# A static planner's engine costs: occupancy apart from latency, with new stage times and a blocked key layout

## The chip, the core and the metric

The kernel runs on one core of a Trainium2 chip. The metric is the device time of one execution in microseconds; before the change it is 1197.02 us, the median of three runs (1195.31 to 1197.02).

## What is computed

The input `x` has 4 sequences of 512 tokens with 128 channels, float32 throughout. Six residual blocks follow each other:

```python
x = x + 0.5 * rwkv_mix(layernorm(x))            # three 128x128 matmuls, token shift, sigmoid, relu^2
x = x + attention(layernorm(x))                 # 16 heads of 64, 512x512 scores, relative bias, softmax
x = x + 0.5 * rwkv_mix(layernorm(x))
x = x + 0.5 * local_transformer(layernorm(x))   # 2 layers
x = x + gated_recurrence(layernorm(x))          # a scan along the tokens, layer norm inside
x = x + 0.5 * local_transformer(layernorm(x))
```

A layer of `local_transformer` is an attention in windows of 64 tokens (8 heads of 64; each query block of 64 sees its own and the previous block: 128 keys), with l2-normalised and rotated q and k, then a feed-forward of 128 to 2 x 341 to 128 with a gelu gate.

## The kernel before

**Work.** Everything is tiled to 128 partitions. The global attention is cut into 32 units, a pair of heads times a sequence (`unit`, L559): q, k and v projections, 4 query tiles of scores, softmax, transposes of the probabilities (one head by TensorE and a ScalarE copy, the other by VectorE, a DRAM buffer and DMAs), the weighted values, and the output projection. A `local_stage` (L877) is one local transformer on one sequence; each of its two layers has 4 token tiles that pass through `rotate`, `values`, `turn`, `soften`, `turn_back`, `weigh`, `turn_outputs` and `project` (L683 to L834), and then `feed_forward`. Each of the 4 sequences has two local stages with a `recurrence` between them and ends in `leave` (transpose, copy, store).

**The key tile.** `turn` (L727) transposes q and k of a token tile with TensorE and copies them out of PSUM with ScalarE. The keys lie in `kT`, [channel, head pair, 64 + 128 tokens]: the first 64 are the previous tile's last 64, brought by one DMA from SBUF to SBUF per tile (48 in all), 4 runs of 64 floats on each partition. `soften` (L746) multiplies each query block of 64 with a run of 128 keys, 16 small matmuls (64x64 weights, 128 columns) to a tile. It then adds the mask (VectorE), takes the maximum (VectorE), subtracts it (GpSimd) and takes the exponential (ScalarE).

**What sets the order.** No instruction is issued as the program is written down. Each is recorded (`Recorder`, L294) as an `Op` with a cost and a due time `vt`; `Plan.plan` (L175) then lays all 5791 ops out, engine by engine, in a greedy list schedule, and `emit` writes them in that order, pinned. The schedule takes the engine that can start first; among the ops that can start on it then, it takes the one with the smallest due time. Ops due later than HORIZON after the oldest unplanned one are passed over. A change of TensorE's tile mode (full array; "row" pairs for the scores; "col" pairs for the weighted values) adds MODE_BIAS to the due time, a change of ScalarE's function table TABLE_BIAS. Buffers (8 PSUM banks, 33 SBUF pairs) are given out in the same walk. So costs and due times decide nothing but the order: the hardware waits on semaphores, whatever the plan thought.

The due times come from a few stage constants on L53 and L54. ATTN is where the units begin; a unit follows the last by 4 STEPs, its later parts are LATER steps behind. LATE is where the local stages begin; TURN is the stride from one turn of a sequence to its next, and the sequences follow each other by LAG turns. The costs come from `Recorder.cost` (L331). In the planner before, an op's cost does two things at once:

```python
free[op.engine] = op.done = at + cost
```

The engine is free, and the result is there, at the same moment.

Of the kernel before, what the change touches and what calls it, by code (L numbers as in the profile page):

```python
# [8 lines left out]
AF = mybir.ActivationFunctionType  # L9
ALU = mybir.AluOpType  # L10
# [4 lines left out]
P = 128  # L15
# [34 lines left out]


PAIRS = 33
STEP, TURN = 3.6, 11.7  # L53
ATTN, LATE, LAG, LATER = 20.5, 400.0, 4.5, 7.7  # L54

class Tile:

# [53 lines left out]
class Op:  # L111
    def __init__(self, engine, vt):
        self.engine, self.vt = engine, vt
        self.calls, self.tiles, self.preds, self.succs = [], [], set(), []
        self.cost, self.mode, self.table, self.bytes = 0.0, None, None, 0
        self.start = self.done = None


class Plan:
# [1 line left out]

    LATENCY, HORIZON, SWITCH, TABLE = 0.07, 31.7, 0.1, 1.28
    IDLE, COLD, FIRST = 2.5, 8.0, 6
    MODE_BIAS, TABLE_BIAS = 10.5, 10.3

    def __init__(self, tc, memory):
        self.tc, self.nc, self.memory = tc, tc.nc, memory
# [45 lines left out]
    def plan(self):  # L175
        for op in self.ops:
            for t in op.tiles:
                t.left += 1
            for p in op.preds:
                p.succs.append(op)  # L180
        for op in reversed(self.ops):
            for s in op.succs:
                op.vt = min(op.vt, s.vt - s.cost)
        waiting = {op: len(op.preds) for op in self.ops}
        ready = {}
        for op in self.ops:
            if not op.preds:
                ready.setdefault(op.engine, []).append((0.0, op))
        free, mode, order, wire, cold = {}, "full", [], 0.0, 0.0
        unplanned = sorted(self.ops, key=lambda o: -o.vt)  # L190
        table = self.FIRST
        while unplanned:
            while unplanned and unplanned[-1].start is not None:
                unplanned.pop()
            if not unplanned:
                break
            horizon = unplanned[-1].vt + self.HORIZON
            best = None
            for engine, ops in ready.items():
                now, able = free.get(engine, 0.0), []  # L200
                for at, op in ops:
                    if op.vt > horizon:
                        continue
                    at = max(at, now)
                    new = [t.kind for t in op.tiles if t.kind != "fixed" and t.slot is None]
                    for kind in set(new):
                        at = max(at, self.memory.when(kind, new.count(kind)))
                    able.append((at, op))
                if not able:
                    continue  # L210
                first = min(a for a, _ in able)
                if best is not None and first >= best[0]:
                    continue
                if first == float("inf"):
                    continue

                def key(x):
                    k = x[1].vt
                    if engine == "tensor" and x[1].mode != mode:
                        k += self.MODE_BIAS  # L220
                    if x[1].table and x[1].table != table:
                        k += self.TABLE_BIAS
                    return k

                at, op = min((x for x in able if x[0] <= first + 0.05), key=key)
                best = (first, at, op)
            if best is None:
                raise RuntimeError("the plan finds no place for anything that is left")
            _, at, op = best
            self.memory.now = at  # L230
            for t in op.tiles:
                if t.kind != "fixed" and t.slot is None:
                    self.memory.take(t)
            op.start, cost = at, op.cost
            if op.engine == "tensor":
                if op.mode != mode:
                    cost, mode = cost + self.SWITCH, op.mode

                if at - free.get("tensor", -self.IDLE) >= self.IDLE:
                    cold = at + self.COLD  # L240
                cost += min(cost, max(0.0, cold - at) / 2)
            if op.table and op.table != table:
                cost, table = cost + self.TABLE, op.table
            free[op.engine] = op.done = at + cost
            if op.bytes:
                wire = max(wire, op.done) + op.bytes / 250e3
                op.done = wire + 2.0
            ready[op.engine] = [x for x in ready[op.engine] if x[1] is not op]
            order.append(op)
            for t in op.tiles:  # L250
                t.left -= 1
                t.end = max(t.end, op.done)
                if not t.left and t.kind != "fixed":
                    self.memory.give(t)
            for s in op.succs:
                waiting[s] -= 1
                if not waiting[s]:
                    at = max(p.done + (self.LATENCY if p.engine != s.engine or p.bytes else 0.0) for p in s.preds)
                    ready.setdefault(s.engine, []).append((at, s))
        return order  # L260
# [33 lines left out]
class Recorder:  # L294
# [36 lines left out]
    def cost(self, name, outs, ins, kw, n):  # L331
# [8 lines left out]
            n = max(v.size() for v in (ins if name == "tensor_reduce" else outs) or outs)  # L340
        if self.engine == "vector":
            if name == "tensor_tensor_scan":
                return 1.22
            if name == "tensor_scalar":
                return 0.15 + 0.0006 * n
            inside = n > 256 and all(v.tile.kind != "S" for v in ins)
            return 0.15 + 0.00105 * n + (0.08 if "accum_out" in kw else 0.0) + 0.3 * inside
        if self.engine == "scalar":
            return 0.12 + 0.0009 * n + (0.32 if "accum_out" in kw else 0.0 if name == "copy" else 0.07)
        if name == "memset":  # L350
            return 0.1 + 0.0008 * n
        return 0.12 + 0.0022 * n + 0.12 * (n == T)


class Memory:
# [63 lines left out]
def tile_macaron(ctx: ExitStack, tc: tile.TileContext, i: dict, out: bass.AP):  # L419
# [47 lines left out]
    def vec(col, n=P):  # L467
        return vecs[:n, col : col + 1]
# [52 lines left out]
    def attention(wo, tdram):  # L521
# [37 lines left out]
        def unit(n, at):  # L559
# [26 lines left out]
            for q in range(NT):  # L586
# [14 lines left out]
                for j in range(2):  # L601
# [7 lines left out]
                    )  # L609
                dve.reciprocal(sm, sm)  # L610
                pool_.tensor_tensor(
                    e, e, sm.unsqueeze(2).to_broadcast([P, 2, T]), ALU.mult, cost=1.92
                )


# [61 lines left out]
    def local_attention(l, h):  # L677
# [5 lines left out]
        def rotate(t):  # L683
# [18 lines left out]

            s3 = sq.rearrange("p (h d) -> p h d", d=DH)
            sh = plan.tile("half", [P, 2 * H1, half])
            pool_.tensor_tensor(sh, s3[:, :, :half], s3[:, :, half:], ALU.add, cost=1.25)
            dve.tensor_reduce(rn, sh, AX.X, ALU.add)

            act.activation(rn, rn, AF.Relu, bias=tiny[:, 0:1])
# [2 lines left out]
            for lo, hi in ((slice(0, half), slice(half, DH)), (slice(half, DH), slice(0, half))):  # L711
                pool_.tensor_tensor(u4[..., lo], u4[..., lo], w4[..., hi], ALU.add, n=INNER)
            u3 = u.rearrange("p (h d) -> p h d", d=DH)
            pool_.tensor_tensor(
                u3, u3, rn.unsqueeze(2).to_broadcast([P, 2 * H1, DH]), ALU.mult, cost=1.94
            )
            us[t] = u

# [8 lines left out]
        def turn(t):  # L727

            u = us.pop(t)
            qTs[t] = plan.tile("half", [P, H1 // 2, P])  # L730

            if t == 0:
                kTs[t] = plan.tile("pair", [P, H1 // 2, WIN + P])
                pool_.memset(kTs[t][:, :, :WIN], 0.0)
            for g, dst in enumerate((qTs[t], kTs[t][:, :, WIN:])):
                ptp = plan.tile("S", [P, H1 // 2, P])
                with plan.bundle(0.44):
                    for pr in range(H1 // 2):
                        c = g * INNER + pr * P
                        pe.transpose(ptp[:, pr, :], u[:, c : c + P], ident)  # L740
                act.copy(dst, ptp, n=T)
            if t + 1 < NT:
                kTs[t + 1] = plan.tile("pair", [P, H1 // 2, WIN + P])
                dma.dma_start(out=kTs[t + 1][:, :, :WIN], in_=kTs[t][:, :, P:])

        def soften(t):  # L746

# [3 lines left out]
            with plan.bundle(0.9, "row"):  # L751
                for pr in range(H1 // 2):
                    for j in range(2):
                        hp = slice(j * DH, (j + 1) * DH)
                        for blk in range(2):
                            c = slice(blk * WIN, (blk + 1) * WIN)
                            pe.matmul(
                                sc[j][c, pr, :], lhsT=qT[hp, pr, c],
                                rhs=kT[hp, pr, blk * WIN : blk * WIN + KEYS], start=True, stop=True,
                            )  # L760
            e = plan.tile("pair", [P, H1, KEYS])
            mask = mask_sb[:, 0 if t == 0 else 1, :].unsqueeze(1).to_broadcast([P, H1 // 2, KEYS])
            for j in range(2):
                dve.tensor_tensor(
                    e[:, j * (H1 // 2) : (j + 1) * (H1 // 2), :], sc[j], mask, ALU.add
                )
            mx = plan.tile("small", [P, H1])
            dve.tensor_reduce(mx, e, AX.X, ALU.max)
            pool_.tensor_tensor(
                e, e, mx.unsqueeze(2).to_broadcast([P, H1, KEYS]), ALU.subtract, cost=1.92  # L770
            )
            act.activation(e, e, AF.Exp)
            es[t] = e

        def turn_back(t):
# [138 lines left out]
    def recurrence(b):  # L914
# [10 lines left out]
        sg = plan.tile("half", [P, T])  # L925
        act.activation(sg, pzh[1], AF.Sigmoid, bias=vec(V_BH))
        ra = plan.tile("half", [P, T])
        dve.tensor_scalar(ra, pzh[1], vec(V_BH), 0.0, ALU.add, ALU.max, cost=0.69)
        dve.scalar_tensor_tensor(ra, sg, 0.5, ra, ALU.min, ALU.add)
        pool_.tensor_tensor(z, z, ra, ALU.mult)  # L930
        plan.step()
# [211 lines left out]
```

## Time and profile before

| | us |
|---|---|
| median of three runs | 1197.02 |
| the profiled execution | 1196.85 |
| its span, first to last instruction | 1195.0 |
| PE busy | 1166.0 |
| VectorE (DVE) busy | 931.7 |
| ScalarE (ACT) busy | 868.1 |
| GpSimd (POOL) busy | 834.6 |

Almost every instruction has the line L313, the recorder's `issue`, so groups have to be told apart by their tiles and shapes. `psS` is a PSUM bank, `pair` any half or whole SBUF work buffer, `small` a small column buffer, `va` and `via` the values and the DRAM buffers. `PEld` is the weight load of a matmul. A float32 matmul stands in the trace as two records, a transpose as one. A matmul's end is modelled, so that PE reads as busy while it may be waiting: times of matmuls are best read from start to start. On the other engines a record runs from the start of an instruction to its last write, and the next one can start before that end.

TensorE's first matmul of an attention unit is at 32.5 us and its last at 498.2; the local stages begin at 406.5, with recurrences between them, and the last sequence's feed-forward and `leave` end the program.

### The profile page before, as it was taken

How to read it: one execution, taken by the hardware profiler on the slowest of the kernel's cores; microseconds unless marked ns; L12 is line 12 of the kernel's file. 1: busy time of each engine (PE TensorE's matmuls, PEld its weight loads, DVE VectorE, ACT ScalarE, POOL GpSimd, SP SyncE). 2: the span in 40 equal slices, each digit the busy share in tenths (PEclk: the TensorE clock that was granted, in tenths of full speed). 3: DMA queues.
4: the chain of work that ended last, by engine and by line, in shares of the span. 5: the costliest groups of instructions: out<-in, count | busy, mean ns of one | idle time of the engine just before them, and what ended most of it. 6: DMA issues, size and time to landing. Idle time of an engine off the chain costs nothing.

```text
span 1195.0 us, 25706 instructions
## 1 busy us (share of the span) xinstructions
PE 1166.0 (98%) x9356; PEld 721.2 (60%) x9356; DVE 931.7 (78%) x1995; ACT 868.1 (73%) x1745; POOL 834.6 (70%) x591
## 2 busy tenths in 40 slices
PE   8999999999999999999999999999999999999996
PEld 3455556565555555567577766664576676776763
DVE  5778778778788787888888787877888888787853
ACT  5887667667676777777777687777877777677772
POOL 4756646656556787999898685726989998786720
PEclk9999999999999999999999999999999999999998
DMA  5276876686885742322021111100121112011100
GB/s 138 92 204 201 247 216 197 199 231 210 227 244 179 227 120 85 89 47 55 14 56 24 45 24 24 45 2 9 28 47 23 42 33 51 15 41 37 41 24 18
DMA packets 98194, 114.97 MB, mean 96 GB/s; under 512 B 33850, under 2 KB 77540, under 8 KB 98068
## 3 DMA queue, kind: packets, MB, share of 16 engines
q1 hardware_dynamic: 97780, 113.24, 33.8%
q8 instruction: 75, 1.23, 0.4%
q14 instruction: 51, 0.42, 0.1%
q10 hardware_dynamic: 288, 0.08, 0.0%
HBM read 57.41 MB, written 43.05 MB: 84 GB/s over the span
## 4 chain that ended last, share of the span: by engine, by line
PE 85%; DVE 7%; POOL 3%; issue 2%; ACT 2%; DMA 1%; SPq 0%; POOLq 0%; DVEq 0%; ACTq 0%
PE psS L313 85%; DVE pair L313 5%; POOL pair L313 3%; ACT pair L313 2%; DVE xT L313 1%; DVE small L313 1%; ACT L283 0%; DMA pair<-in_x_dram 0%; DMA pair<-via 0%; DVE w L313 0%; SPq L313 0%; POOLq L1139 0%; ACT small L313 0%; POOLq L313 0%; DVEq L313 0%
## 5 line engine op out<-in xcount | busy, mean ns | idle before, releaser
L313 POOL TENSOR_TENSOR pair<-pair,small 128x1024 f32<-128x1024 f32 x256 | 484.4, 1907 | 208.3 <-DVE small L313 168.2
L313 ACT COPY pair<-psS 128x512 f32<-128x512 f32 (+1 forms) x518 | 284.0, 590 | 136.5 <-PE psS L313 122.6
L313 PE MATMUL psS<-pair,pair 64*64 64x128 f32 (+4 forms) x4508 | 370.5, 300 | 2.3 <-ACT pair L313 1.0
L313 PEld LDWEIGHTS psS<-pair,pair 128*64 128x64 f32 (+2 forms) x4508 | 246.9, 140 | 116.6 <-issue 33.7
L313 PEld LDWEIGHTS psS<-ident,pair 128*128 128x128 f32 x1808 | 210.4, 142 | 117.5 <-issue 87.8
L313 POOL TENSOR_TENSOR pair<-pair,pair 128x512 f32<-128x512 f32 (+1 forms) x177 | 226.3, 1294 | 73.7 <-ACT pair L313 62.1
L313 PE MATMUL psS<-ident,pair 128*128 128x128 f32 x1808 | 248.4, 276 | 8.3 <-DMA pair<-in_x_dram 4.8
L313 ACT ACTIVATE pair<-pair,small 128x512 f32<-128x512 f32 x256 | 181.9, 712 | 43.7 <-DVE small L313 39.7
L313 DVE CUSTOM_DVE_ANT_0 pair<-psS,pair 128x512 f32<-128x512 f32 x256 | 164.7, 684 | 40.5 <-PE psS L313 40.1
L313 PE MATMUL psS<-wqkv,pair 128*128 128x512 f32 x384 | 185.6, 600 | 0.3 <-DVE pair L313 0.2
L313 POOL TENSOR_TENSOR pair<-pair 128x512 f32<-128x512 f32 x87 | 109.5, 1261 | 58.7 <-ACT pair L313 50.1
L313 ACT ACTIVATE pair<-pair 128x512 f32<-128x512 f32 (+1 forms) x152 | 122.3, 812 | 33.6 <-DVE pair L313 16.8
L313 PE MATMUL psS<-pair,w 128*128 128x512 f32 (+2 forms) x288 | 132.0, 604 | 3.8 <-POOL pair L313 3.5
L313 PE MATMUL psS<-pair 64*128 64x512 f32 (+2 forms) x548 | 128.0, 589 | 0.0
L313 DVE TENSOR_REDUCE small<-pair 128x16 f32<-128x512 f32 (+1 forms) x128 | 120.2, 948 | 6.2 <-POOL pair L313 4.0
L313 DVE TENSOR_TENSOR pair<-psS,cos 128x512 f32<-128x512 f32 x128 | 87.5, 684 | 37.0 <-PE psS L313 22.8
L313 ACT ACTIVATE pair<-psS 128x512 f32<-128x512 f32 x144 | 81.8, 596 | 45.5 <-PE psS L313 20.4
L313 PEld LDWEIGHTS psS<-wqkv,pair 128*128 128x128 f32 x384 | 65.4, 190 | 52.0 <-issue 42.9
L313 DVE TENSOR_TENSOR pair<-psS,sin 128x512 f32<-128x512 f32 x128 | 87.1, 681 | 11.4 <-ACT pair L313 11.3
L313 PEld LDWEIGHTS psS<-pair,w 128*128 128x128 f32 (+2 forms) x288 | 51.4, 185 | 67.2 <-issue 53.9
L313 DVE TENSOR_TENSOR pair<-psS,mask 128x512 f32<-128x512 f32 x128 | 82.6, 684 | 12.0 <-PE psS L313 8.0
L313 DVE STREAM_TRANSPOSE pair<-pair 128x512 f32<-128x512 f32 x128 | 87.5, 697 | 4.5 <-POOL pair L313 2.6
(71 smaller groups left out, 1183.6 us busy)
## 6 DMA issues: line engine op xcount, KB each, us to landing
via<-pair SPq DMA_DIRECT2D x64, 512.0 KB, 3.0
pair<-via SPq DMA_DIRECT2D x256, 128.0 KB, 3.5
pair<-va SPq DMA_DIRECT2D x112, 130.0 KB, 2.4
table<-tdram SPq DMA_DIRECT2D x16, 511.5 KB, 6.9
pair<-table SPq DMA_DIRECT2D x16, 448.0 KB, 5.2
pair<-pair SPq DMA_DIRECT2D x48, 128.0 KB, 2.3
wqkv<-in_L_ffn_wqkv_dram SPq DMA_DIRECT2D x2, 768.0 KB, 6.5
pair<-in_x_dram SPq DMA_DIRECT2D x4, 256.0 KB, 3.6
```

The source lines that it names most:

```text
L313: real(*[a.resolve() if isinstance(a, View) else a for a in args], **{k: a.resolve() if isinstance(a, View) else a for k, a in kw.items()},)
```

## The change

The planner now has two numbers for an op of VectorE, ScalarE and GpSimd: `cost`, for which the engine is held, and a TAIL after it, until which the result isn't there. The cost formulas of these engines are new, the explicit costs too, and so are eight stage constants (STEP, TURN, ATTN, LATE, LAG, LATER, HORIZON, TABLE_BIAS). Apart from the order, one thing that is executed changes: the key tile is kept in blocks of 32 tokens, [channel, block, head pair, 32], so that the previous tile's last 64 keys are one run of 256 floats on each partition. The key copy writes, and the score matmul reads, 4 runs of 32 floats where it was one of 128. `mx` is named earlier in the program and `scale=1.0` is written out at an exponential. The number of instructions of each engine stays what it was, but for ScalarE's table loads, which the order decides.

```diff
-STEP, TURN = 3.6, 11.7
-ATTN, LATE, LAG, LATER = 20.5, 400.0, 4.5, 7.7
+STEP, TURN = 3.5, 9.982
+ATTN, LATE, LAG, LATER = 14.455, 401.778, 3.886, 9.94
...
-    LATENCY, HORIZON, SWITCH, TABLE = 0.07, 31.7, 0.1, 1.28
+    LATENCY, HORIZON, SWITCH, TABLE = 0.07, 33.081, 0.1, 1.28
...
+    TAIL = {"vector": 0.085, "scalar": 0.115, "gpsimd": 0.05}
-    MODE_BIAS, TABLE_BIAS = 10.5, 10.3
+    MODE_BIAS, TABLE_BIAS = 10.5, 10.538
...
-            free[op.engine] = op.done = at + cost
+            free[op.engine] = at + cost
+            op.done = at + cost + self.TAIL.get(op.engine, 0.0)
...
             if name == "tensor_tensor_scan":
-                return 1.22
-            if name == "tensor_scalar":
-                return 0.15 + 0.0006 * n
-            inside = n > 256 and all(v.tile.kind != "S" for v in ins)
-            return 0.15 + 0.00105 * n + (0.08 if "accum_out" in kw else 0.0) + 0.3 * inside
+                return 1.2
+            psum = any(v.tile.kind == "S" for v in ins)
+            lo, hi = (outs + ins)[0].region()[0]
+            if name == "tensor_tensor_reduce":
+                return 0.078 + 0.00104 * n
+            inside = len(ins) > 1 and n > 256 and not psum
+            return 0.064 + 0.00104 * n + 0.09 * (hi - lo <= 64) + 0.06 * (len(ins) > 2) + 0.3 * inside
         if self.engine == "scalar":
-            return 0.12 + 0.0009 * n + (0.32 if "accum_out" in kw else 0.0 if name == "copy" else 0.07)
+            if name == "copy":
+                return 0.04 + 0.00083 * n
+            wide = len(ins) > 1 or any(v.tile.kind != "S" for v in ins)
+            return 0.05 + 0.00083 * n + 0.09 * wide + 0.06 * ("accum_out" in kw)
...
-        return 0.12 + 0.0022 * n + 0.12 * (n == T)
+        return 0.1 + 0.0022 * n
...
-                    e, e, sm.unsqueeze(2).to_broadcast([P, 2, T]), ALU.mult, cost=1.92
+                    e, e, sm.unsqueeze(2).to_broadcast([P, 2, T]), ALU.mult, cost=1.86
...
+            def keys():
+                return plan.tile("pair", [P, 2 + NQ, H1 // 2, QU])
             if t == 0:
-                kTs[t] = plan.tile("pair", [P, H1 // 2, WIN + P])
-                pool_.memset(kTs[t][:, :, :WIN], 0.0)
+                kTs[t] = keys()
+                pool_.memset(kTs[t][:, :2], 0.0)
...
+            act.copy(
+                kTs[t][:, 2:].rearrange("p a h u -> p h a u"),
+                ptp.rearrange("p h (a u) -> p h a u", u=QU), n=T,
+            )
             if t + 1 < NT:
-                kTs[t + 1] = plan.tile("pair", [P, H1 // 2, WIN + P])
-                dma.dma_start(out=kTs[t + 1][:, :, :WIN], in_=kTs[t][:, :, P:])
+                kTs[t + 1] = keys()
+                dma.dma_start(
+                    out=kTs[t + 1][:, :2].rearrange("p a h u -> p (a h u)"),
+                    in_=kTs[t][:, NQ:].rearrange("p a h u -> p (a h u)"),
+                )
...
-                                rhs=kT[hp, pr, blk * WIN : blk * WIN + KEYS], start=True, stop=True,
+                                rhs=kT[hp, blk * 2 : blk * 2 + 4, pr, :], start=True, stop=True,
```

The other explicit costs of GpSimd go from 1.92 to 1.86, 1.94 to 1.86 and 1.25 to 1.12, and an explicit 0.69 of a VectorE op gives way to the formula.

More of the change, by code (lines that the diff above doesn't have):

```diff
@@ L114, in __init__ @@
         self.calls, self.tiles, self.preds, self.succs = [], [], set(), []
-        self.cost, self.mode, self.table, self.bytes = 0.0, None, None, 0
+        self.cost, self.mode, self.table, self.bytes, self.tail = 0.0, None, None, 0, 0.0
         self.start = self.done = None
 class Plan:
-    LATENCY, HORIZON, SWITCH, TABLE = 0.07, 31.7, 0.1, 1.28
+    LATENCY, HORIZON, SWITCH, TABLE = 0.07, 33.081, 0.1, 1.28
     IDLE, COLD, FIRST = 2.5, 8.0, 6
-    MODE_BIAS, TABLE_BIAS = 10.5, 10.3
+    TAIL = {"vector": 0.085, "scalar": 0.115, "gpsimd": 0.05}
+    MODE_BIAS, TABLE_BIAS = 10.5, 10.538
     def __init__(self, tc, memory):
@@ L704, in rotate @@
             sh = plan.tile("half", [P, 2 * H1, half])
-            pool_.tensor_tensor(sh, s3[:, :, :half], s3[:, :, half:], ALU.add, cost=1.25)
+            pool_.tensor_tensor(sh, s3[:, :, :half], s3[:, :, half:], ALU.add, cost=1.12)
             dve.tensor_reduce(rn, sh, AX.X, ALU.add)
@@ L714, in rotate @@
             pool_.tensor_tensor(
-                u3, u3, rn.unsqueeze(2).to_broadcast([P, 2 * H1, DH]), ALU.mult, cost=1.94
+                u3, u3, rn.unsqueeze(2).to_broadcast([P, 2 * H1, DH]), ALU.mult, cost=1.86
             )
@@ L730, in turn @@
             qTs[t] = plan.tile("half", [P, H1 // 2, P])
+            def keys():
+                return plan.tile("pair", [P, 2 + NQ, H1 // 2, QU])
             if t == 0:
-                kTs[t] = plan.tile("pair", [P, H1 // 2, WIN + P])
-                pool_.memset(kTs[t][:, :, :WIN], 0.0)
[L735 to L741, printed above, removed]
-            if t + 1 < NT:
-                kTs[t + 1] = plan.tile("pair", [P, H1 // 2, WIN + P])
-                dma.dma_start(out=kTs[t + 1][:, :, :WIN], in_=kTs[t][:, :, P:])
+                kTs[t] = keys()
+                pool_.memset(kTs[t][:, :2], 0.0)
+            ptp = plan.tile("S", [P, H1 // 2, P])
+            with plan.bundle(0.44):
+                for pr in range(H1 // 2):
+                    pe.transpose(ptp[:, pr, :], u[:, pr * P : (pr + 1) * P], ident)
+            act.copy(qTs[t], ptp)
+            ptp = plan.tile("S", [P, H1 // 2, P])
+            with plan.bundle(0.44):
+                for pr in range(H1 // 2):
+                    c = INNER + pr * P
+                    pe.transpose(ptp[:, pr, :], u[:, c : c + P], ident)
+            act.copy(
+                kTs[t][:, 2:].rearrange("p a h u -> p h a u"),
+                ptp.rearrange("p h (a u) -> p h a u", u=QU), n=T,
+            )
+            if t + 1 < NT:
+                kTs[t + 1] = keys()
[3 more added lines that the diff above has]
+                )
         def soften(t):
@@ L758, in soften @@
                                 sc[j][c, pr, :], lhsT=qT[hp, pr, c],
-                                rhs=kT[hp, pr, blk * WIN : blk * WIN + KEYS], start=True, stop=True,
+                                rhs=kT[hp, blk * 2 : blk * 2 + 4, pr, :], start=True, stop=True,
                             )
             e = plan.tile("pair", [P, H1, KEYS])
-            mask = mask_sb[:, 0 if t == 0 else 1, :].unsqueeze(1).to_broadcast([P, H1 // 2, KEYS])
+            mask = mask_sb[:, 0 if t == 0 else 1, :]
+            mx = plan.tile("small", [P, H1])
+            mask = mask.unsqueeze(1).to_broadcast([P, H1 // 2, KEYS])
             for j in range(2):
@@ L766, in soften @@
                 )
-            mx = plan.tile("small", [P, H1])
             dve.tensor_reduce(mx, e, AX.X, ALU.max)
             pool_.tensor_tensor(
-                e, e, mx.unsqueeze(2).to_broadcast([P, H1, KEYS]), ALU.subtract, cost=1.92
+                e, e, mx.unsqueeze(2).to_broadcast([P, H1, KEYS]), ALU.subtract, cost=1.86
             )
-            act.activation(e, e, AF.Exp)
+            act.activation(e, e, AF.Exp, scale=1.0)
             es[t] = e
@@ L927, in recurrence @@
         ra = plan.tile("half", [P, T])
-        dve.tensor_scalar(ra, pzh[1], vec(V_BH), 0.0, ALU.add, ALU.max, cost=0.69)
+        dve.tensor_scalar(ra, pzh[1], vec(V_BH), 0.0, ALU.add, ALU.max)
         dve.scalar_tensor_tensor(ra, sg, 0.5, ra, ALU.min, ALU.add)
```

## The prediction

> **What bounds the kernel.** I read the page first.
>
> ```profile
> span 1195.0 us, 25706 instructions
> ...
> PE 1166.0 (98%) x9356; PEld 721.2 (60%) x9356; DVE 931.7 (78%) x1995; ACT 868.1 (73%) x1745; POOL 834.6 (70%) x591
> ...
> PE   8999999999999999999999999999999999999996
> ...
> POOL 4756646656556787999898685726989998786720
> PEclk9999999999999999999999999999999999999998
> ...
> PE 85%; DVE 7%; POOL 3%; issue 2%; ACT 2%; DMA 1%; SPq 0%; POOLq 0%; DVEq 0%; ACTq 0%
> ```
>
> TensorE carries the chain, but its 98% is not 98% of its peak, since a matmul's end is modelled. So I took the trace's starts. Undisturbed, a 128x512 record starts 0.429 us after the last (1108 of them, 475.3 us), a transpose 0.110 (1824, 199.7), a 128x128 record 0.111 (768, 85.2); of the tiled bundles a score pair takes 0.858 (128, 109.8), the local scores of a tile 0.874 (64, 55.9), eight weighted-value matmuls 1.727 (64, 110.5), eight local ones 0.466 (128, 59.6); the bias matmuls 2.6. Sum 1098.9 us. Each unbroken run of tiled bundles costs 0.15 to 0.20 more (a single score pair takes 1.059 to the next start, four take 3.634, so 0.20 is fixed): 35 score runs, 39 weighted, 41 local-score (0.16) and 39 local-weighted runs (0.15), 25.3 us. With 4.2 us to the first matmul and 4.1 after the last, 1132.5. The other 62.5 us are waits of TensorE: up to 75 us 10.4; between 375 and 525, where units give way to local stages, 10.5; between 750 and 925, where recurrences give way to the second local stages, 14.8; from 1100 on 12.8; elsewhere small ones, 14.0 in all.
>
> The end, in order of time (start, us, engine, operation, tiles, idle time before):
>
> ```profile
> 1170.63 1.05 PE L313 MATMUL psS<-pair,wo 128*128 128x128 f32 x8
> ...
> 1172.38 1.13 PE L313 MATMUL psS<-pair,ones 128*128 128x512 f32 x2
> ...
> 1175.02 1.12 PE L313 MATMUL psS<-pair,ones 128*128 128x512 f32 x2 [1.51 <-ACT pair L313]
> ...
> 1177.70 1.26 POOL L313 TENSOR_TENSOR pair<-pair,pair 128x512 f32<-128x512 f32 x1 [16.71 <-ACT pair L313]
> ...
> 1179.02 10.58 PE L313 MATMUL psS<-pair,w 128*128 128x512 f32 x18 [2.88 <-POOL pair L313]
> ...
> 1190.44 0.66 PE L313 MATMUL psS<-ident,xT 128*128 128x128 f32 x4 [0.85 <-DVE xT L313]
> ```
>
> One sequence is alone: after its last projection (1170.63) the two layer-norm matmuls, GpSimd's multiply and the feed-forward wait for one another. The clock falls as well, as the view by stretches shows (PE, PEld, DVE, ACT, POOL busy, granted clock):
>
> ```profile
> 1178.00:1185.00 7.00, 5.98 (x8) 2.43 (x9) 0.00 (x0) 2.81 (x4) 0.96 (x1) 0.55 0.00 0
> ```
>
> At 0.55 six records stand 0.857 apart, not 0.429: 2.6 us.
>
> **The premise.** Is an engine free before its result is there? First the group of ScalarE's copies (count, busy, mean ns), then two of them in order of time:
>
> ```profile
> L313 ACT COPY pair<-psS 128x512 f32<-128x512 f32 x516 | 282.9, 590 | 136.4 <-PE psS L313 122.6 <-DVE pair L313 6.1 <-DVE small L313 5.1
> ```
>
> ```profile
> 212.97 1.07 ACT L313 COPY pair<-psS 128x512 f32<-128x512 f32 x2 [2.72 <-PE psS L313]
> ```
>
> One copy takes 590 ns, two in a row 1.07 us: the second starts 0.48 after the first. The old formula holds ScalarE for 0.58 us, the new one for 0.465 with a result at 0.58. By starts likewise, VectorE's 128x512 from PSUM lasts 0.684 and is followed after 0.598 (old 0.688, new 0.596 + 0.085); GpSimd's 128x512 after 1.23 (old 1.37, new 1.23 + 0.05), its 128x1024 after 1.85 (old 1.92, new 1.86). The new costs are what this trace shows. They save no engine time; they decide which op the planner believes it can place next, and the gain can only come out of the 62.5 us of waits and 25.3 us of mode runs.
>
> **Part by part**, from the order of the changed program; a position is TensorE's work so far at the rates above, and another engine's work is counted between the TensorE steps that the plan puts it among. The counts of PE, DVE, POOL and SP instructions are equal (5592, 1997, 596, 571); so the 1098.9 us stay.
>
> *Mode runs.* 35, 39, 41, 39 become 33 score, 33 weighted, 38 local-score and 35 local-weighted runs: 2 x 0.20 + 6 x 0.15 + 3 x 0.16 + 4 x 0.15 = 2.4 us less on TensorE. It is the bound, so nothing covers that.
>
> *The end.* Before, the order behind the last projection is the other sequence's leave, layer norm, layer norm, six feed-forward matmuls, w2, leave: 10.3 us of TensorE work, all but 0.44 of it one chain. Now the last projection stands 7.7 us of work earlier (position 1080.1 of 1099, not 1087.8), and between the layer norm's two matmuls lie six matmuls of the sequence before (5.15 us), behind the second its w2 and leave (3.0). With this trace's latencies from that projection: 0.88 + 0.87 wait + 0.86 + 5.15 + 0.3 (its own wait for GpSimd) + 0.86 + 2.58 + 1.0 (wait for x) + 0.44; the normalised input is ready (ScalarE 1.3, GpSimd 1.3) before that ends; then 5.15 + 2.58, and 6.0 to the end as before: 26.7 us. Before, the same work begins at 1162.4 + 0.1 and ends at 1195.0: 32.5 us. Saved 5.8; I take 5.4, for a wait in the crowded 20 us ahead (its bounds: 2, if VectorE is late with the projections, and 7). About half is clock. A rule bears on that. The Trainium skill (TensorE: Matmul & The Clock Gate, Part 1) halves the clock after an idle window of some 3.4 us and advises gaps under 3 us; here it fell with no gap over 2.9 in the row above. By the row a gap of 2.9 us is already dear; by the rule it is free, the fall was another's doing and may come again, and only 2.8 us are saved. I go by the row: the new end's gaps are near 1 us.
>
> *The middle* (work positions 700 to 870). For the 14.8 us the chain in order of time (start, us) names GpSimd:
>
> ```profile
> 821.33 4.19 POOL pair L313 x3
> ...
> 828.80 3.19 POOL pair L313 x3
> ...
> 845.15 1.91 POOL pair L313
> ```
>
> Its work is bunched by the rotations of the second local stages. Priced by the spacings above, the old order gives it 11.6 us in 40 of TensorE's from 720 to 760, then 95.9 in 100 (780 to 880); the new one 9.4, then 99.7. So the bunch is not spread. What gets better: the last recurrence ends at position 809 rather than 819, the last feed-forward ahead of it at 772 rather than 783. ScalarE's table loads (1.28 each) are 61, not 59, but 15 rather than 10 between positions 700 and 780; its work there, loads included, is 61.8 us in 80 (before 60.5), so they hide. I take -3, between +5 (GpSimd fuller) and -10.
>
> *The handover* (375 to 525 us, 10.5). Units end at position 455 (457), rwkv at 472 (472); GpSimd has 17 to 20 us of work in each 20 of TensorE's, before 16.5 to 19. I take -2, between +4 and -7. *Start:* the first sequences' layer norms are as serial as before, with a matmul or two moved between: -0.5 (+1 to -2). *The 14.0 of small waits*, each some 0.1 to 0.4 us and due to a result believed early or an engine believed busy: -2, between +14 and -7.
>
> *The key tile.* The copy writes 32-float runs, as the attention's copies do, which share the 590 ns row. Its DMA has a quarter of the packets (48 x 384 fewer of 98194); it lands in 2.3 us, a tile ahead of its reader, on a queue with DMA shares of 0.1 to 0.2: 0 (bounds -1 and +1). The score matmul streams 4 runs of 32. Against that speaks the Trainium skill (Advanced Engine Details and Errata, PSUM Cachelines): any non-contiguous access slows matmuls significantly. The nearest row streams runs of 64 out of a strided tile: 8 matmuls of 256 columns take 1.727 us, just as many streamed columns as two 512 score pairs' contiguous 2 x 0.858. By the row 0; by the rule, were it half speed, 64 x 0.874 = 56 us. I take 0, as the stride is in SBUF, and PSUM is written in one run. `scale=1.0`, `mx` and the other queues' orders: no work added, 0.
>
> Sum: -2.4 - 5.4 - 3 - 2 - 0.5 - 2 = -15.3. The profiled execution took 1196.85, 1.85 over its span; that gives 1181.55, and with the median 0.17 above it 1181.7.
>
> **Rivals.** (1) The gain stays at the end and in the mode runs; middle and handover bunch as before: -7.8, 1189. The bunch counts speak for it. Chance 0.19, of it 0.03 within 0.2%. (2) The better costs empty the waits widely: -2.4 - 5.4 - 10 - 7 - 0.5 - 5 = -30.3, 1167. For it: most engine costs were 10 to 25% off. Against: GpSimd. 0.15. (3) Slower: the plan now packs engines at their bare spacing, and whatever runs late (table loads, GpSimd's 128x1024, 1.907 mean) makes TensorE wait throughout. Price: the small waits double, +14, and middle and handover go to their upper ends, +5 and +4, against -7.8: +15, 1212. It decides from 8 us of new waits, under 1% of the span. 0.12. (4) Strided keys at half speed: 1237; they decide from 0.25 us to a bundle. 0.03. That the plan hardly changes is excluded: the PE order differs almost throughout.
>
> **Numbers.** The likeliest case (1175 to 1187) 0.51. A measurement of this kernel tells 0.2% (2.4 us) from none. Faster: 0.51 + 0.15 + 0.16 of (1) = 0.82. The same: the 0.03 of (1) and 0.02 of (3), which can stop at its turning point. Slower: 0.10 of (3) and 0.03 of (4). Range 1165 to 1197: it takes in (1) and (2) and leaves out most of (3), (4).
>
> **What would show it.** Right: no half clock after 1100 and feed-forward matmuls 0.43 apart at the end; last projection to end under 28 us; matmul starts still 0.429 apart, local scores 0.874 a bundle; waits by stretch 5 us less at the end, a few less in the middle and the handover. Wrong: local scores above 1 us a bundle; small waits above 22 us; GpSimd's chain in the middle longer than the 26 us from 821 to 847.

## The result: 0.45% slower, and the profile after

The changed kernel takes 1201.83 us (median of four, 1201.38 to 1202.33); in the same comparison the kernel before took 1196.84. The ratio is 1.0045, 95% interval [1.0027, 1.0062]. The prediction was 1181.7 us and faster; it was wrong in sign. The span, from the first instruction to the last, grew by 3.8 us of these 5 in the profiled executions. The rest lies outside it: the four runs of the changed kernel have 2.6 to 3.6 us there, all others in this document 1.7 to 2.0. Why stays open.

The page after, lines as in the prediction:

```profile
span 1198.8 us, 25618 instructions
...
PE 1158.2 (97%) x9356; PEld 722.8 (60%) x9356; DVE 914.0 (76%) x1995; ACT 856.5 (71%) x1747; POOL 833.6 (70%) x591
...
PEclk9999999999999999999999999999999999999999
```

TensorE's busy time fell by 8 us while the span grew by 4: its work stands further apart. The starts of the matmuls, less the same rates as in the prediction, tell where (us of TensorE waiting, by stretch of the span; the runs e5, e9 and e10 are explained below):

| | before | after | e5 | e9 | e10 |
|---|---|---|---|---|---|
| 0 to 75 | 10.4 | 12.0 | 11.4 | 11.2 | 10.8 |
| 75 to 375 | 5.3 | 4.7 | 4.7 | 4.7 | 5.3 |
| 375 to 525 | 10.5 | 11.1 | 10.2 | 10.9 | 10.6 |
| 525 to 750 | 5.1 | 10.7 | 5.1 | 4.7 | 4.6 |
| 750 to 925 | 14.8 | 14.1 | 13.0 | 12.9 | 11.9 |
| 925 to 1100 | 3.7 | 8.1 | 4.9 | 4.3 | 4.1 |
| 1100 to the end | 12.8 | 7.7 | 5.2 | 6.1 | 9.9 |
| sum | 62.5 | 68.5 | 54.5 | 54.7 | 57.1 |
| mode runs | 25.3 | 22.9 | 23.0 | 22.9 | 25.3 |

Mode runs give 2.4 us and the end 5.1; the two stretches in which only local stages run, quiet before, lose 5.6 and 4.4 (10.7 - 5.1 and 8.1 - 3.7), the start 1.6.

The end, TensorE in order of time:

```profile
1170.83 2.20 PE L316 MATMUL psS<-pair,wo 128*128 128x128 f32 x16
...
1173.73 1.13 PE L316 MATMUL psS<-pair,ones 128*128 128x512 f32 x2 [0.70 <-DVE pair L316]
1174.69 5.31 PE L316 MATMUL psS<-pair,w 128*128 128x512 f32 x12
1179.84 1.02 PE L316 MATMUL psS<-pair,ones 128*128 128x512 f32 x2
1180.70 2.74 PE L316 MATMUL psS<-pair,w 128*128 128x512 f32 x6
...
1184.28 0.66 PE L316 MATMUL psS<-ident,xT 128*128 128x128 f32 x4 [0.84 <-DVE xT L316]
1184.94 8.00 PE L316 MATMUL psS<-pair,w 128*128 128x512 f32 x18
```

and by stretches (granted clock third from the end):

```profile
1178.00:1185.00 7.00, 6.16 (x18) 2.51 (x16) 3.00 (x4) 3.29 (x6) 1.27 (x1) 1.00 0.00 0
```

Twelve matmul records of the sequence before lie between the two of the layer norm, the clock stays full, and the last 18 records take 8.00 us where they took 10.58.

The new wait shows in a rotation. VectorE first, then ScalarE, in the same two microseconds (in brackets the idle time before, and what ended it):

```profile
434.17 0.69 DVE L316 TENSOR_TENSOR pair<-psS,cos 128x512 f32<-128x512 f32 x1
435.52 0.69 DVE L316 TENSOR_TENSOR pair<-psS,sin 128x512 f32<-128x512 f32 x1 [0.66 <-ACT pair L316]
```

```profile
434.89 1.08 ACT L316 ACTIVATE pair<-psS 128x512 f32<-128x512 f32 x2 [0.18 <-DVE pair L316]
```

`rotate` reads one projected half of q or k in PSUM three times: VectorE multiplies it by cos and by sin, ScalarE squares it. Between its two multiplies VectorE stands still for 0.66 us although its input is there: it waits for ScalarE's square, which itself began only when the first multiply was over. The built program has both waits as semaphores. These are its lines for this half, in the order of the plan's starts:

```
TensorTensor pair16_127<-psS6_69,cos0_179 128x512 [waits PE_49]
Activation pair15_126<-psS6_69 128x512 [waits DVE_49]
TensorTensor pair14_125<-psS6_69,sin0_180 128x512 [waits Activation_49]
```

Both engines only read. But in the traces of before and after, ScalarE's and VectorE's records on one bank overlap for 0 us in all 128 halves: one engine at a time reads a bank, and I call this the exclusion. The planner knows only dependencies in which at least one side writes. So it plans these reads side by side: by 31 us in 65 halves before, by 41 us in 87 halves after.

### The profile page after: what moved, and what is told of

It is laid out like the page before. It is cut to its first block, busy times and chain, and to the rows that moved or that the text cites. A ratio compares the mean times of both kernels' runs of the same rounds, so it can differ in the third digit from the quotient of the medians.

```text
span 1198.8 us, 25618 instructions
## 1 busy us (share of the span) xinstructions
PE 1158.2 (97%) x9356; PEld 722.8 (60%) x9356; DVE 914.0 (76%) x1995; ACT 856.5 (71%) x1747; POOL 833.6 (70%) x591
## 2 busy tenths in 40 slices
DMA packets 79760, 114.94 MB, mean 96 GB/s; under 512 B 9274, under 2 KB 59108, under 8 KB 79636
## 5 line engine op out<-in xcount | busy, mean ns | idle before, releaser
L316 ACT COPY pair<-psS 128x512 f32<-128x512 f32 (+1 forms) x518 | 278.6, 594 | 138.6 <-PE psS L316 134.9
L316 PE MATMUL psS<-pair,pair 64*64 64x128 f32 (+4 forms) x4520 | 366.7, 300 | 1.1 <-DVE pair L316 0.6
L316 PEld LDWEIGHTS psS<-pair,pair 128*64 128x64 f32 (+2 forms) x4520 | 249.9, 140 | 122.7 <-issue 51.5
L316 PEld LDWEIGHTS psS<-ident,pair 128*128 128x128 f32 x1808 | 207.1, 142 | 98.5 <-issue 67.1
L316 PE MATMUL psS<-ident,pair 128*128 128x128 f32 x1808 | 238.0, 275 | 13.2 <-DMA pair<-in_x_dram 4.0
L316 POOL TENSOR_TENSOR pair<-pair 128x512 f32<-128x512 f32 (+1 forms) x87 | 108.2, 1245 | 59.1 <-ACT pair L316 50.0
L316 PE MATMUL psS<-pair 64*128 64x512 f32 (+1 forms) x536 | 124.9, 593 | 0.0
L316 ACT ACTIVATE pair<-psS 128x512 f32<-128x512 f32 x144 | 82.6, 601 | 48.8 <-PE psS L316 23.3
L316 PEld LDWEIGHTS psS<-wqkv,pair 128*128 128x128 f32 x384 | 67.8, 192 | 68.8 <-issue 47.6
L316 DVE TENSOR_TENSOR pair<-psS,sin 128x512 f32<-128x512 f32 x128 | 87.4, 683 | 21.9 <-ACT pair L316 21.9
L316 DVE STREAM_TRANSPOSE pair<-pair 128x512 f32<-128x512 f32 x128 | 89.1, 698 | 16.1 <-POOL pair L316 15.9
```

What stands on the lines that cost most here:

```text
L316: real(*[a.resolve() if isinstance(a, View) else a for a in args], **{k: a.resolve() if isinstance(a, View) else a for k, a in kw.items()},)
```

## How far the chip falls behind the plan

The planner computes a start for every op while it lays out the order, so the trace can be laid beside its plan. The plan's own end, the span of the profiled execution, and the lag, which is the second less the first (us):

| | plan's end | span | lag |
|---|---|---|---|
| before | 1180.6 | 1195.0 | 14.5 |
| after | 1161.0 | 1198.8 | 37.8 |
| e2, costs alone | 1169.2 | 1207.2 | 37.9 |
| e3, stage times alone | 1196.7 | 1208.7 | 12.0 |
| e4, TensorE tail | 1172.7 | 1209.0 | 36.3 |
| e5, bank rule | 1162.1 | 1184.7 | 22.6 |
| e6, bank rule in before | 1181.0 | 1191.0 | 10.1 |
| e7, bank rule and tail | 1174.1 | 1195.4 | 21.4 |
| e8, STEP 3.52 | 1162.3 | 1197.2 | 34.9 |
| e11, found | 1164.9 | 1180.2 | 15.3 |
| e12, bank rule, SBUF cost | 1166.3 | 1187.8 | 21.5 |

The change did what it was made for: its plan is 19.5 us shorter. The chip then fell 23.3 us further behind it. I followed the trace back from the last instruction over what each step had waited for, and took the growth of the lag at each. A first count put 15 of some 37 us after the change on VectorE in the rotations, and 9.5 between a rotation's matmul and VectorE. With the waits between two readers of a bank as steps of their own, 22.7 of 37.9 us arise at these after the change, and 6.5 of 14.6 before.

## The experiments

My first theory (A) was that a plan packed on bare engine spacings leaves the chip no slack, with TensorE's results, which have no tail in the plan, as the likeliest cause. B was the key tile, C that any new order draws a new time by chance. D, the exclusion on the bank, came after the first four runs. Ratios are to the kernel before.

**e1, the key tile alone** (before, with `turn` and `soften` of the change; of its edit, the line of the score matmul).

```diff
-                                rhs=kT[hp, pr, blk * WIN : blk * WIN + KEYS], start=True, stop=True,
+                                rhs=kT[hp, blk * 2 : blk * 2 + 4, pr, :], start=True, stop=True,
```

> The kernel before with the blocked key tile alone; order, costs and stage times as before. Theory A (the loss is in the order: a plan packed on bare engine spacings that the chip can't follow): 1197 us, within 2 us of before, and 0.874 us to a bundle of local scores. Theory B (the strided keys or their copies cost the time): about 1202, score bundles longer. Theory C (any new order of this program falls anywhere within some 8 us): as A, 1197, since the order is not touched.

1196.13 us, 0.9996 [0.9988, 1.0005]. The order is untouched, TensorE's waits in the trace are 63.1 us (62.5 before), and where two local-score bundles follow each other, the second starts a median 0.924 us after the first, in the traces of before, e1 and after alike. The strided keys cost nothing that can be measured; B falls.

**e2, costs alone** (after, with the old stage constants).

```diff
-STEP, TURN = 3.5, 9.982
-ATTN, LATE, LAG, LATER = 14.455, 401.778, 3.886, 9.94
+STEP, TURN = 3.6, 11.7
+ATTN, LATE, LAG, LATER = 20.5, 400.0, 4.5, 7.7
...
-    LATENCY, HORIZON, SWITCH, TABLE = 0.07, 33.081, 0.1, 1.28
+    LATENCY, HORIZON, SWITCH, TABLE = 0.07, 31.7, 0.1, 1.28
...
-    MODE_BIAS, TABLE_BIAS = 10.5, 10.538
+    MODE_BIAS, TABLE_BIAS = 10.5, 10.3
```

> The changed kernel with the old stage times: new costs and tails, new key tile. The plan's own end is 1169 us here, 1161 with the new stage times, 1181 before; the chip ended 14.5 us after the plan before, 37.8 us after it with the change. Theory A: the lag comes with the new costs, so some 30 to 38 us of it are kept: 1200 to 1207 us. The stage times as culprit: near or below before, under 1192. Theory C: anywhere between 1190 and 1207.

1208.24 us, 1.0100 [1.0085, 1.0115], lag 37.9; the time is 1.2 us above theory A's range.

**e3, stage times alone** (before, with the reverse of that edit).

> The kernel before with the new stage times alone; its plan ends at 1197 us by the old costs. Theory A: the old costs keep the lag near 10 to 15 us, so 1207 to 1212, slower than both; the small waits away from the ends stay near 14 us and the time is lost elsewhere. If the stage times were good by themselves: 1185 to 1197. Theory C: anywhere between 1195 and 1212.

1211.12 us, 1.0126 [1.0110, 1.0141], lag 12.0. Taken with e2, the lag goes with the costs. The new stage times are worth 8.2 us of plan under the new costs (1169.2 to 1161.0); under the old ones the plan is 16.1 us longer with them (1180.6 to 1196.7).

**e4, a tail for TensorE.**

```diff
-    TAIL = {"vector": 0.085, "scalar": 0.115, "gpsimd": 0.05}
+    TAIL = {"tensor": 0.17, "vector": 0.085, "scalar": 0.115, "gpsimd": 0.05}
```

> The changed kernel with one number more in its TAIL: 0.17 us for TensorE, whose results the plan believes to be there the moment the array is free, while in the trace of the changed kernel VectorE starts 0.27 and ScalarE 0.21 after that (0.07 of it planned). The plan ends at 1173 us. Theory A: the lag falls from 38 to about 20 to 25 us and the small waits of the local stages (18.9 us) by a third or more: 1193 to 1198. Theory C: no better than chance, 1190 to 1207, the lag still above 28.

1211.08 us, 1.0124 [1.0100, 1.0148]; the lag is 36.3 us. My first cause fails: the tail is real (in the trace after, VectorE starts 0.20 to 0.27 us after TensorE is free where nothing else holds it, and the plan has 0.07) but it isn't what the lag is made of. This sent me to the growth of the lag step by step, and to the bank.

**e5, the bank rule** in the changed kernel's planner.

```diff
+                    for t in op.tiles:
+                        if t.kind == "S" and engine != "tensor":
+                            at = max([at] + [end + self.LATENCY for e, end in t.reads.items() if e != engine])
...
+            for t in op.tiles:
+                if t.kind == "S" and op.engine != "tensor":
+                    t.reads[op.engine] = op.done
```

> The changed kernel, and its planner is told one thing more: ScalarE and VectorE don't read one PSUM bank at the same time (an op waits in the plan for the end of the other engine's planned reads of its bank). In the traces so far these reads never overlap, since each waits on the other's semaphore, while the plan of the changed kernel overlaps them in 87 of 128 halves of the rotations (65 before), and the steps at which the chip falls behind that plan lie there (15 us on VectorE behind a rotation, 9.5 between its matmul and VectorE, of 37). The plan's end stays at 1162 us. Theory D (this unplanned exclusion makes the lag): the lag falls from 38 to 15 to 22, so 1177 to 1184 us, and the small waits of the local stages from 18.9 to about 10. Theory A (no slack anywhere, whatever the cause): the lag stays above 30, 1193 or more. Theory C (chance): between 1190 and 1207.

1186.67 us, 0.9915 [0.9900, 0.9930]: 1.3% less than the change (0.9915 / 1.0045; the profiled spans differ by 14.1 us), from a plan that ends 1.1 us later. The small waits of the local stages go from 18.9 to 10.0 us (5.1 + 4.9), as expected; the lag falls to 22.6, just above what was expected, and the time is 2.7 us above it. The multiply by sin, after:

```profile
L316 DVE TENSOR_TENSOR pair<-psS,sin 128x512 f32<-128x512 f32 x128 | 87.4, 683 | 21.9 <-ACT pair L316 21.9
```

and with the rule:

```profile
L323 DVE TENSOR_TENSOR pair<-psS,sin 128x512 f32<-128x512 f32 x128 | 87.0, 679 | 0.2 <-POOL pair L323 0.2
```

(idle time before the group, and what ended it.) The exclusion is still there, but ScalarE's square now falls between the two multiplies in 2 of the 128 halves, after the change in 29.

**e6, the bank rule in the kernel before.**

> The kernel before with the same rule in its planner, old costs and stage times; plan's end 1181 us in both. Theory D: its costs were too long by 0.1 to 0.4 us an op, which left room for the exclusion: of its lag of 14.5 us only some 3 steps' worth lies at rotations, so 1192 to 1197. Theory C: anywhere between 1190 and 1207.

1193.41 us, 0.9976 [0.9964, 0.9989]. As expected: the old order loses little to the exclusion.

**e7, bank rule and tail.**

> The changed kernel with the bank rule and the 0.17 us tail of TensorE; plan's end 1174 us. Theory D: the lag falls further than by the rule alone, to 8 to 15: 1182 to 1189, the later plan eating what the smaller lag gives. Theory A or C: above 1200, as with the tail alone.

1195.46 us, 0.9998 [0.9986, 1.0010]. Neither fits: the lag of 21.4 us is that of the rule alone, so the tail bought nothing, and the plan it led to is 12 us longer.

**e8, another draw** (STEP 3.5 to 3.52).

> The changed kernel with STEP at 3.52 instead of 3.5: plan's end 1162.3 us, 203 of 1464 TensorE steps elsewhere. It measures how far a new draw of the order moves the time. Theory C: 4 us or more from the changed kernel's 1201.8. Theories A and D: the lag stays at 35 to 41, so 1198 to 1204.

1198.98 us, 1.0023 [1.0015, 1.0032], lag 34.9. This new draw of the order moves the time by some 3 us (the spans by 1.6), so C is not nothing: single differences of that size between these versions say little. The 15 us of e5 are beyond it.

**e9, the exclusion taken away, the order kept.** The planner sees the same op; at issue ScalarE's square reads a weight in SBUF, so this kernel leaves out the norms of q and k.

```diff
-                act.activation(sq[:, c], pq, AF.Square)
+                seen = View(pq.tile)
+                seen.stand_in = wqkv[:, :INNER].resolve()
+                act.activation(sq[:, c], seen, AF.Square)
```

> The changed kernel in its own order, instruction by instruction; only ScalarE's square in the rotation reads 512 columns of a weight in SBUF instead of the PSUM bank that VectorE reads too, so neither waits for the other there. (The norms of q and k are left out so: their squares are those of weights.) Theory D (the exclusion on the shared bank is what the new plan loses to): 15 to 22 us less than the changed kernel's 1201.8, so 1180 to 1187, like the bank rule without changing any plan. Theory A (lack of slack in general): under 6 us less, 1196 or more.

1186.97 us, 0.9924 [0.9907, 0.9940]; 1.2% less than the change, with the engines' orders equal op by op. The sin multiplies:

```profile
L318 DVE TENSOR_TENSOR pair<-psS,sin 128x512 f32<-128x512 f32 x128 | 87.0, 680 | 0.0
```

Their 21.9 us of waiting are gone, the squares and the multiplies run side by side for 34 us, and TensorE's waits in the two quiet stretches fall from 18.9 to 9.0 us.

But e9 takes away more than the exclusion: a square that reads a weight need not wait for its projection either. ScalarE's group of squares, after and in e9:

```profile
L316 ACT ACTIVATE pair<-psS 128x512 f32<-128x512 f32 x144 | 82.6, 601 | 48.8 <-PE psS L316 23.3 <-DVE pair L316 22.1 <-issue 3.2
```

```profile
L318 ACT ACTIVATE pair<-wqkv 128x512 f32<-128x512 f32 x128 | 75.7, 637 | 3.9 <-PE psS L318 2.5 <-issue 1.4
```

Here 48 of the 128 squares begin before their projection is done. To part the two, I replayed the trace of the changed kernel: every engine keeps its order, and every op its measured time and its measured delay behind what released it; only waits between the reads of a rotation are dropped. This is an estimate from that trace: the span falls by 13.3 us, to 1185.5 (e9: 1185.1), and by 0.1 more if the squares also need not wait for their projections. (For the kernel before the replay gives 1191.6, where e10 below measured 1189.5.) With the exclusion kept and only the squares freed it falls by 2.1. So D is shown as the main part of the loss: by an order that avoids the exclusion (e5), by a kernel without it (e9), and by the replay, which takes the exclusion alone.

The same replay, as an estimate of what the exclusion costs elsewhere: 3.4 us before and 3.1 in e1; 8.3 in e3; 13.1 to 16.5 in e2, e4 and e8, as after the change; at most 0.8 in all runs whose planner has the bank rule.

**e10, the same in the kernel before.**

> The kernel before in its own order, with ScalarE's square reading a weight in SBUF as in e9 (the norms of q and k left out in the same way). Theory D: the old order lost little to the exclusion, 2 to 5 us: 1191 to 1194; the changed order lost 15, and the difference of the two is what turned a shorter plan into a longer run. Against it: 10 us or more here too, which would leave the two orders as far apart as they were.

1191.58 us, 0.9969 [0.9956, 0.9982]: 0.31% to gain here, against 1.2% in the changed order. Without the exclusion the new order is the faster one, 0.9924 against 0.9969; with it, the slower. The faster by 5.4 us, though, not by the 15.3 forecast: about what rival (1) left, the end and the mode runs.

**e11, the version found**: the bank rule, the tail, the SBUF cost of e12, and stage constants chosen anew under them by the plan's end.

```diff
-STEP, TURN = 3.5, 9.982
-ATTN, LATE, LAG, LATER = 14.455, 401.778, 3.886, 9.94
+STEP, TURN = 3.500, 9.779
+ATTN, LATE, LAG, LATER = 14.079, 400.675, 3.877, 10.744
...
-    LATENCY, HORIZON, SWITCH, TABLE = 0.07, 33.081, 0.1, 1.28
+    LATENCY, HORIZON, SWITCH, TABLE = 0.07, 41.104, 0.1, 1.28
...
-    MODE_BIAS, TABLE_BIAS = 10.5, 10.538
+    MODE_BIAS, TABLE_BIAS = 10.337, 10.536
```

> The version that the experiments point to: bank rule, a tail of 0.17 us for TensorE, 0.65 instead of 0.3 us added for VectorE's two-input operations within SBUF (planned 0.96 to 0.99, in the traces 2.0 to 2.4 where GpSimd runs beside them), and all stage constants chosen anew under these costs; plan's end 1165 us. Theory D: a lag of 12 to 20, so 1179 to 1187 after the 2 us around the span, the same as or faster than the bank rule alone. Theory C: anywhere between 1180 and 1200.

1183.04 us, 0.9894 [0.9877, 0.9911], lag 15.3. It beats both kernels; from e5 its interval does not part it ([0.9900, 0.9930]). TensorE's waits are 49.7 us, with 6.9 in the handover, where the kernels of the table above have 10.2 to 11.1.

**e12, bank rule and SBUF cost.**

```diff
-            return 0.064 + 0.00104 * n + 0.09 * (hi - lo <= 64) + 0.06 * (len(ins) > 2) + 0.3 * inside
+            return 0.064 + 0.00104 * n + 0.09 * (hi - lo <= 64) + 0.06 * (len(ins) > 2) + 0.65 * inside
```

> The bank rule with the longer SBUF cost, stage constants of the changed kernel; plan's end 1166 us, 4 later than with the bank rule alone. If those operations make the rest of the lag (22.5 us with the bank rule): a lag of 14 to 18, so 1182 to 1186; if they don't: the lag stays, 1190.

1190.32 us, 0.9951 [0.9936, 0.9966]; the lag stays at 21.5. What the rest of the lag is made of stays open: it is not the exclusion (0.8 us in e5 and 0.3 here, by the replay), and neither this cost nor TensorE's tail (e7) cures it alone.

## Why the prediction was wrong, point by point

- **Mode runs, -2.4.** Right: 33, 33, 38 and 35 runs in the trace, 22.9 us against 25.3.
- **The end, -5.4.** Right: -5.1, no half clock while matmuls run, 27.0 us from the last projection (1171.87) to the end (26.7 worked out).
- **The middle, -3; the handover, -2; the start, -0.5.** -0.7, +0.6 and +1.6: all too hopeful, the first two inside their bounds, the start 0.6 outside. GpSimd's bunch stayed, as the prediction and rival (1) had it. What lengthens the start stays open.
- **The small waits, -2, between +14 and -7.** This is the step that failed: +9.5 us (23.6 in the three quiet stretches, before 14.0), past the 22 that the prediction had named as a sign of being wrong. Its sign came from "The new costs are what this trace shows", from which I let a better plan follow. The costs are right for the groups that were checked. What the plan lacks is a constraint, the exclusion. e9 puts its price after the change at 13.7 us of span and the replay at 13.3, more than the loss itself; before, the replay has 3.4. Costs too long by 0.1 to 0.4 us an op had hidden most of that lack: under the old costs the replay's price is 3.1 to 8.3 us, under the new ones 13.1 to 16.5. Why the padding shields the rotations so well is argued, not shown.
- **Rival (3)** named the place (small waits throughout, +14) and was given 0.12; its cause was wrong. Not table loads nor GpSimd's 128x1024, but a wait between two readers.
- **It could have been read before.** The group of sin multiplies of the kernel before:

```profile
L313 DVE TENSOR_TENSOR pair<-psS,sin 128x512 f32<-128x512 f32 x128 | 87.1, 681 | 11.4 <-ACT pair L313 11.3
```

The second of two multiplies of the same input, one after the other on one engine, has nothing to wait for but its output buffer; 11.3 us of waiting for ScalarE were the missing constraint, in sight. In 27 of the 128 halves before, the square already fell between the two multiplies.
- **The key tile, 0.** Right (e1), and packets fell by 18434 where 18432 were counted (98194 to 79760). The rule weighed there would have cost 56 us at half speed; 32-float runs in SBUF cost nothing measurable (0.9996 [0.9988, 1.0005]).
- **The half clock.** It went with the gaps at the end, as the row of before suggested: the five kernels with the old stage constants (before, e1, e2, e6, e10) have 3.4 to 6.8 us of half clock while the end's matmuls run, all others none there. No run changes the gaps alone. The reading that a gap under 3 us is free does not hold elsewhere in the changed kernel either: here the clock halves right behind a gap of 1.97 us (granted clock third from the end).

```profile
871.52 1.68 PE L316 MATMUL psS<-xT,ones 128*128 128x512 f32 x2 [1.97 <-DVE xT L316]
```

```profile
872.00:875.00 3.00, 3.00 (x5) 1.31 (x4) 3.00 (x4) 2.63 (x7) 3.00 (x2) 0.50 0.00 0
```

- **The sums.** The parts of the 1098.9 us add up to 1098.6; nothing hangs on it.

## What to carry to other kernels

Before a static scheduler gets tighter costs, lay its planned starts beside a trace and find the steps at which the lag grows: a constraint that it does not know can cost little under padded costs and much under exact ones (here 3 to 8 us against 13 to 17). In the view by groups, look for a wait that the dependencies of the program do not explain. A shorter plan is a shorter run only if the lag stays what it was.

## What was not expected of the hardware

- In every trace here in which they read the same bank, ScalarE and VectorE never do so at the same time, though nothing was written: 0 us of overlap in 128 halves. The wait is a semaphore in the built program, so the runs do not show what the chip would do without it; that was not tried.
- VectorE's 128x512 scalar_tensor_tensor with all inputs in SBUF takes 0.75 us (25.24 in the trace before, no GpSimd operation beside it) and up to 2.4 us beside GpSimd's (452.16 in the trace after), where both planners have 0.96 to 0.99. e12 shows that pricing this in does not by itself help.
